# Layer 0 of an attention pair: denominators and output projection put off to the end of the next block

## The chip, the cores and the metric

The kernel runs on one core of a Trainium2 chip. The metric is the device time of one execution in microseconds, the median of several runs; one further execution was recorded by the hardware profiler. Engines are named as in the profile: PE is TensorE (PEld its weight loads), DVE VectorE, ACT ScalarE, POOL GpSimd. All data are fp32.

## The reference

Four images x of 128 channels and 64 x 64 positions (N = 4096) pass two layers. What matters here:

```python
# layer 0: attention over all positions, 64 channels inside
q, k, v = wq @ x, wk @ x, wv @ x                      # 64 x N each
att = softmax(k.T @ q, axis=2)                        # N x N
x = x + wo @ (v @ att.T)                              # projection back to 128 channels
# layer 1: tokens t = x transposed (N x 128)
h = layernorm(t)
t = t + causal_softmax(h Wq (h Wk).T / sqrt(128)) @ (h Wv)
t = t + recurrent_ffn(layernorm(t))                   # batch norm, then a scan over tokens
```

## The kernel before

For each of the four batches, layer 0 handles eight blocks of 512 rows, then layer 1 eight blocks. A block is a list of items; a layer-0 item is two key tiles of 128 (16 items a block), and its scores and values are 64x64 matmuls that occupy the four quarters of the PE array. Layer 1 uses 128x128 matmuls. The softmax isn't normalized until the end: exp of the scores is summed on DVE (`dsum`), and the sums of a block (`den`) are transposed, reduced and inverted later.

PSUM pools: `ps_s` has two score tiles, `ps_a` one accumulator `acc`, and `ps_m` two tiles for everything else; `misc(name)` takes one of the latter, and a tile is free again when its last reader is through.

```python
def misc(name):
    return ps_m.tile([P, BLK], F32, tag="m", name=name)      # pool ps_m: bufs=2
```

The tools' build puts the instructions of each engine into a fixed order, which need not be the order of the source.

The end of a layer-0 block: `acc` is copied out and added up (`agg`), the sums too (`den`); two slots later `project` turns them into the new tokens.

```python
def project(layer, b, g, agg, den):
    dp = misc("den_ps")
    for j in range(TPB):                                        # 4 transposes
        nc.tensor.transpose(dp[:, ts(j, P)], den[:, ts(j, P)], ident)
    rec = recs[:, layer, b, ts(g, TPB)]
    nc.vector.tensor_reduce(rec, dp.rearrange("p (j k) -> p j k", k=P), AX.X, ALU.add)
    nc.vector.reciprocal(rec, rec)
    op = misc("o_ps")
    for j in range(TPB):                                        # 4 matmuls 128x128
        nc.tensor.matmul(op[:, ts(j, P)], lhsT=agg[:, ts(j, P)], rhs=wv1 if layer else wo2, ...)
    for j in range(TPB):
        t = xs[:, b, ds(g * BLK + j * P, P)]
        nc.vector.scalar_tensor_tensor(t, in0=op[:, ts(j, P)], scalar=rec[:, j : j + 1], in1=t, ...)

def transposed(src, dst, name, engine):
    ps = misc(name)
    for j in range(TPB):                                        # 4 transposes
        nc.tensor.transpose(ps[:, ts(j, P)], src[:, j], ident)
    engine(dst, ps)

def finish0(b, g):                                              # layer 0
    agg, den = bs[b].agg, bs[b].den
    ...
    yield 2, lambda: (project(0, b, g, agg, den), norm())       # two slots after the block's end
    fill.append(lambda: transposed(bs[b].xh[...], bs[b].xhT[...], "xhT_ps", nc.scalar.copy))

def values(it):
    ...                                                         # matmuls into bt.acc
    if it.last:
        bt.agg = wk.tile([P, BLK], F32, tag="agg", name="agg")
        if it.layer == 0:
            half = wk.tile([P, 2, BLK], F32, tag="half", name="half")
            nc.scalar.copy(half, bt.acc)
            nc.vector.tensor_tensor(bt.agg, half[:, 0], half[:, 1], ALU.add)
        else:
            nc.scalar.copy(bt.agg, bt.acc[:, 0])
        bt.den = wk.tile([P, BLK], F32, tag="den", name="den")
        nc.vector.tensor_tensor(bt.den, it.den[:, 0], it.den[:, 1], ALU.add)
```

The loop over slots runs scores two items ahead of values:

```python
for s in range(len(items) + SKEW + 16):
    ...
    scores(items[s])                    # PE scores, ACT exp
    it = items[s - SKEW]
    values(it)                          # PE values
    if it.last:
        rows()                          # rows of the block after next; for layer 1 a matmul into r_ps
        if fill:
            fill.pop(0)()               # norm transposes of the preceding block
        push(s, (finish1 if it.layer else finish0)(it.b, it.g))
    sums(items[s])                      # DVE: dsum += p
    ...                                 # then one piece of work that is due
```

So a layer-0 block's projection and layer norm run early in the next block, and the transposes of its normed tokens at the end of that next block.

Of the kernel before, what the change touches and what calls it, by code (L numbers as in the profile page):

```python
# [9 lines left out]
F32 = mybir.dt.float32  # L10
AF = mybir.ActivationFunctionType
ALU = mybir.AluOpType
# [3 lines left out]
P = 128  # L16
BLK = 512
# [325 lines left out]
def fast_path(  # L343
# [21 lines left out]
    nc = tc.nc  # L365
    B, C, N = x.shape
    M = c_wqT.shape[1]
    assert C == P and M == P // 2 and N % CHUNK == 0
    NT = N // P
    NB = N // BLK  # L370
    TPB = BLK // P
# [52 lines left out]
    recs = const.tile([P, 2, B, NT], F32, name="recs")  # L424
# [10 lines left out]
    with tc.tile_pool(name="batch", bufs=1) as batch, tc.tile_pool(name="rows", bufs=2) as rowp, tc.tile_pool(  # L435
        name="prob", bufs=4
    ) as prob, tc.tile_pool(name="work", bufs=2) as wk, tc.tile_pool(name="stat", bufs=4) as stat, tc.tile_pool(
        name="ps_s", bufs=2, space=PSUM
    ) as ps_s, tc.tile_pool(name="ps_a", bufs=1, space=PSUM) as ps_a, tc.tile_pool(
        name="ps_m", bufs=2, space=PSUM  # L440
    ) as ps_m:

        def misc(name):
            return ps_m.tile([P, BLK], F32, tag="m", name=name)
# [69 lines left out]
            nc.vector.tensor_copy(r, ps)  # L514
            bs[b].next.append(r)

        def project(layer, b, g, agg, den):

            dp = misc("den_ps")
            for j in range(TPB):  # L520
                nc.tensor.transpose(dp[:, ts(j, P)], den[:, ts(j, P)], ident)  # L521
            rec = recs[:, layer, b, ts(g, TPB)]
            nc.vector.tensor_reduce(rec, dp.rearrange("p (j k) -> p j k", k=P), AX.X, ALU.add)
            nc.vector.reciprocal(rec, rec)
            op = misc("o_ps")
            for j in range(TPB):
                nc.tensor.matmul(  # L527
                    op[:, ts(j, P)], lhsT=agg[:, ts(j, P)], rhs=wv1 if layer else wo2, start=True, stop=True
                )
            for j in range(TPB):  # L530
                t = xs[:, b, ds(g * BLK + j * P, P)]
                nc.vector.scalar_tensor_tensor(  # L532
                    t, in0=op[:, ts(j, P)], scalar=rec[:, j : j + 1], in1=t, op0=ALU.mult, op1=ALU.add
                )

        def normed(b, g, dst):

            st = stat.tile([P, TPB, nc.vector.BN_STATS_DIM], F32, tag="st", name="ln_st")
            mv = stat.tile([P, TPB, nc.vector.BN_AGGR_DIM], F32, tag="mv", name="ln_mv")
            for j in range(TPB):  # L540
                nc.vector.bn_stats(st[:, j], xs[:, b, ds(g * BLK + j * P, P)])  # L541
                nc.vector.bn_aggr(mv[:, j], st[:, j])
            var = stat.tile([P, TPB], F32, tag="var", name="ln_var")
            nc.vector.tensor_scalar(var, mv[:, :, 1], LN_EPS, None, ALU.add)  # L544
            y = stat.tile([P, TPB], F32, tag="rstd", name="ln_rstd")
            rsqrt(y, var, stat.tile([P, TPB], F32, tag="z", name="ln_z"))
            for j in range(TPB):
                nc.vector.tensor_scalar(  # L548
                    dst[:, j], xs[:, b, ds(g * BLK + j * P, P)], mv[:, j, 0:1], y[:, j : j + 1], ALU.subtract, ALU.mult
                )  # L550
# [14 lines left out]
            nc.vector.tensor_tensor(r, r, r2, ALU.mult)  # L565
            nc.vector.tensor_reduce(good, r, AX.X, ALU.add)

        def finish0(b, g):

            agg, den = bs[b].agg, bs[b].den  # L570

            def norm():
                if g == 0:
                    bs[b].xh = batch.tile([P, NT, P], F32, tag="xh", name="xh")
                    bs[b].xhT = batch.tile([P, N], F32, tag="xhT", name="xhT")
                normed(b, g, bs[b].xh[:, ts(g, TPB)])

            yield 2, lambda: (project(0, b, g, agg, den), norm())
            fill.append(
                lambda: transposed(bs[b].xh[:, ts(g, TPB)], bs[b].xhT[:, ts(g, BLK)], "xhT_ps", nc.scalar.copy)  # L580
            )

        def finish1(b, g):
            agg, den = bs[b].agg, bs[b].den
            mem = {}

            def first():
                project(1, b, g, agg, den)
                mem["xh"] = wk.tile([P, TPB, P], F32, tag="xh2", name="xh2")
                normed(b, g, mem["xh"])  # L590

            def second():
                t = xs[:, b, ts(g, BLK)].rearrange("p (j c) -> p j c", c=P)
                xc = wk.tile([P, BLK], F32, tag="xc", name="xc")
                transposed(t, xc, "tT_ps", nc.scalar.copy)
                nc.sync.dma_start(out=x2[b, :, ts(g, BLK)], in_=xc)
                mem["xhT"] = wk.tile([P, BLK], F32, tag="xhT2", name="xhT2")
                transposed(mem["xh"], mem["xhT"], "xh2T_ps", nc.vector.tensor_copy)

            def third():  # L600
                wp = misc("wx_ps")
                nc.tensor.matmul(wp, lhsT=wf, rhs=mem["xhT"], start=True, stop=True)  # L602
                if b == B - 1 and g == NB - 1:
                    in_range()
                nc.vector.bn_stats(stats[:, b * NB + g], wp)  # L605

                nc.scalar.copy(  # L607
                    xs[:, b, ts(g, BLK)].rearrange("p (s c) -> p s c", c=CPB),
                    wp.rearrange("p (c s) -> p s c", s=STEPS),
                )  # L610

            yield 1, first
            yield 3, second
            yield 1, third
# [84 lines left out]
        def values(it):  # L699

            bt = bs[it.b]
            if it.first:
                bt.acc = ps_a.tile([P, 2, BLK], F32, tag="a", name="acc")
            for h, (t, q0, n, o) in enumerate(it.at):
                if it.layer == 0:

                    for r in range(2):
                        part = slice(r * M, r * M + M)
                        nc.tensor.matmul(  # L709
                            bt.acc[h * M : h * M + M, r],  # L710
                            lhsT=bt.v[part, t],
                            rhs=it.p[part, o : o + n],
                            start=it.first,
                            stop=it.last,
                        )
                else:
                    nc.tensor.matmul(  # L717
                        bt.acc[:, 0, q0:],
                        lhsT=bt.xh[:, t],
                        rhs=it.p[:, o : o + n],  # L720
                        start=it.first and h == 0,
                        stop=it.last and h == 1,
                    )
            if it.last:
                bt.agg = wk.tile([P, BLK], F32, tag="agg", name="agg")
                if it.layer == 0:
                    half = wk.tile([P, 2, BLK], F32, tag="half", name="half")
                    nc.scalar.copy(half, bt.acc)  # L728
                    nc.vector.tensor_tensor(bt.agg, half[:, 0], half[:, 1], ALU.add)
                else:  # L730
                    nc.scalar.copy(bt.agg, bt.acc[:, 0])
                bt.den = wk.tile([P, BLK], F32, tag="den", name="den")
                nc.vector.tensor_tensor(bt.den, it.den[:, 0], it.den[:, 1], ALU.add)

        waiting = []
        fill = []

        def push(slot, chain):
            step = next(chain, None)
            if step:  # L740
                waiting.append((slot + step[0], step[1], chain))
# [13 lines left out]
        side = []  # L755

        def rows():

            if blocks:
                layer, b, g = blocks.pop(0)  # L760
                (rows1 if layer else rows0)(b, g)
                if layer == 0:
                    tokens0(b, g)
# [3 lines left out]
        for s in range(len(items) + SKEW + 16):  # L767
            if s < len(items):
                it = items[s]
                if it.first:  # L770
                    bs[it.b].rows = bs[it.b].next.pop(0)
                    if it.layer and it.g == 1 and it.b + 1 < B:
                        for m in range(NB // 2):
                            side += keys(it.b + 1, m)
                scores(it)
            if 0 <= s - SKEW < len(items):
                it = items[s - SKEW]
                values(it)
                if it.last:
                    rows()  # L780
                    if fill:
                        fill.pop(0)()
                    push(s, (finish1 if it.layer else finish0)(it.b, it.g))
            if s < len(items):
                sums(items[s])
            due = [w for w in waiting if w[0] <= s]
            if due:
                w = min(due, key=lambda w: w[0])
                waiting.remove(w)
                w[1]()  # L790
                push(s, w[2])
            elif side:
                side.pop(0)()
        assert not waiting and not side and not fill

# [143 lines left out]
```

## Time and profile before

| | |
|---|---|
| time, median of 3 runs | 2187.38 us (2187.21 to 2190.06) |
| span of the profiled execution | 2186.7 us |
| granted TensorE clock, mean | 0.989 |
| PE scores, layer 0 (L649) | 4096 instructions, mean 593 ns |
| PE values, layer 0 (L709) | 4096 instructions, mean 590 ns |
| PE transposes den_ps (L521), both layers | 256 instructions, 40.2 us busy |
| PE projection o_ps (L527), layer 0 | 256 instructions, 33.8 us busy |
| PE norm transposes xhT_ps (L556) | 128 instructions, 20.4 us busy |
| ACT copy half (L728) | 32 instructions, about 1003 ns each |
| DVE reduction of den_ps (L523) | 64 instructions, about 684 ns each |
| DVE running sum dsum (L689) | 676 instructions, mean 1225 ns |

Busy time is the sum in which an engine has some instruction at work. The chain that ended last is read backwards from the last instruction, at each step to what released it; its share by engine says who sets the end. A detailed line of the timeline gives start, duration, engine, source line, operation, output and inputs, and in brackets how long the engine had been idle and what ended that. An fp32 matmul that isn't a transpose stands as two instructions in the records.

### The profile page before, as it was taken

The page shows a single profiled execution, that of the slowest core. Times are in us where ns is not written, and L with a number is a line of the kernel's source. Part 1 is how long each engine was busy: PE and PEld are TensorE (multiplying, and loading weights), DVE is VectorE, ACT ScalarE, POOL GpSimd, SP SyncE. Part 2 cuts the span into 40 slices and gives each one's busy share as a digit, 9 for nine tenths or more (in the row PEclk, how much of TensorE's full clock was granted, in tenths as well). Part 3 has the DMA queues.
Part 4 walks back from the last instruction along what each step waited for, and adds up shares of the span by engine and source line. Part 5 has one row for each costly group of instructions (what it writes and reads, how often), then busy time and mean ns, then how long its engine had stood idle before and what let it go on. Part 6 is the DMA issues. An engine that isn't in the chain of part 4 may idle for free.

```text
span 2186.7 us, 30521 instructions
## 1 busy us (share of the span) xinstructions
PE 2113.2 (97%) x12204; PEld 939.7 (43%) x12204; DVE 1440.6 (66%) x2703; ACT 1057.2 (48%) x1162; POOL 104.5 (5%) x207
## 2 busy tenths in 40 slices
PE   6999999999999999999999999999999999999973
PEld 2333354444333345444333335444433334544452
DVE  3888865444788875544688876445478887544486
ACT  4666633333566643333466653332366664332378
POOL 0000010000000010000000001000000001000000
PEclk9999999999999999999999999999999999999986
DMA  6000011000000001000000001100000000000033
GB/s 222 1 1 1 1 31 47 5 6 5 6 1 1 1 20 39 20 10 5 6 1 1 1 1 39 39 6 5 5 6 1 1 1 6 10 10 6 5 159 155
DMA packets 30134, 48.74 MB, mean 22 GB/s; under 512 B 3104, under 2 KB 20256, under 8 KB 28448
## 3 DMA queue, kind: packets, MB, share of 16 engines
q1 hardware_dynamic: 28096, 46.15, 6.1%
q8 instruction: 98, 1.61, 0.3%
q10 hardware_dynamic: 1888, 0.56, 0.1%
q14 instruction: 52, 0.43, 0.1%
HBM read 25.72 MB, written 16.78 MB: 19 GB/s over the span
## 4 chain that ended last, share of the span: by engine, by line
PE 92%; ACT 4%; DVE 2%; DMA 1%; POOL 0%; issue 0%; ACTq 0%; DVEq 0%
PE s_ps L658 21%; PE acc L717 21%; PE s_ps L649 20%; PE acc L709 19%; PE o_ps L527 2%; ACT yt L853 1%; PE den_ps L521 1%; PE kr_ps L469 1%; PE wx_ps L602 1%; ACT xs L841 1%; PE r_ps L512 1%; PE xhT_ps L556 1%; PE v_ps L481 1%; ACT y L841 1%; DVE dsum L689 1%; PE xh2T_ps L556 1%
## 5 line engine op out<-in xcount | busy, mean ns | idle before, releaser
L689 DVE TENSOR_TENSOR dsum<-dsum,p 128x1024 f32<-128x1024 f32 x676 | 828.0, 1225 | 465.6 <-ACT p L665 336.7
L663 ACT ACTIVATE p<-s_ps,nshift 128x1024 f32<-128x1024 f32 x512 | 571.2, 1116 | 354.8 <-PE s_ps L649 335.3
L665 ACT ACTIVATE p<-s_ps 128x1024 f32<-128x1024 f32 (+2 forms) x288 | 274.2, 952 | 564.0 <-PE s_ps L658 462.5
L709 PE MATMUL acc<-p,v 64*64 64x512 f32 x4096 | 532.3, 590 | 1.7 <-ACT half L728 1.7
L649 PE MATMUL s_ps<-swap,kr 64*64 64x512 f32 x2048 | 528.2, 593 | 0.4 <-ACT p L663 0.4
L649 PE MATMUL s_ps<-kr 64*64 64x512 f32 x2048 | 528.2, 593 | 0.0
L658 PE MATMUL s_ps<-rows,xhT 128*128 128x512 f32 (+3 forms) x1152 | 503.9, 559 | 0.0
L717 PE MATMUL acc<-p,xh 128*128 128x512 f32 (+3 forms) x1152 | 501.5, 557 | 0.0
L717 PEld LDWEIGHTS acc<-p,xh 128*128 128x128 f32 x1152 | 215.6, 190 | 241.3 <-issue 231.8
L658 PEld LDWEIGHTS s_ps<-rows,xhT 128*128 128x128 f32 x1152 | 211.0, 190 | 227.1 <-issue 189.7
L709 PEld LDWEIGHTS acc<-p,v 64*64 64x64 f32 x4096 | 155.1, 133 | 284.6 <-issue 265.6
L649 PEld LDWEIGHTS s_ps<-swap,kr 64*64 64x64 f32 x2048 | 136.9, 133 | 130.9 <-issue 123.9
L649 PEld LDWEIGHTS s_ps<-kr 64*64 64x64 f32 x2048 | 137.0, 133 | 128.3 <-issue 123.7
L429 POOL TENSOR_TENSOR ln_rstd<-ln_var,mhalf 128x4 f32<-128x4 f32 x64 | 66.1, 1033 | 1218.6 <-DVE ln_var L544 1218.6
L697 DVE TENSOR_TENSOR dsum<-dsum,p 128x256 f32<-128x256 f32 (+1 forms) x120 | 56.1, 500 | 72.4 <-POOL p L669 72.4
L687 DVE COPY dsum<-p 128x1024 f32<-128x1024 f32 x60 | 41.4, 690 | 67.3 <-ACT p L665 57.6
L532 DVE SCALAR_TENSOR_TENSOR xs<-o_ps,recs,xs 128x128 f32<-128x128 f32 x256 | 73.0, 345 | 8.9 <-PE o_ps L527 2.8
L548 DVE TENSOR_SCALAR xh<-xs,ln_mv,ln_rstd 128x128 f32<-128x128 f32 x256 | 71.4, 343 | 2.2
L669 POOL TENSOR_SCALAR_AFFINE_SELECT p<-p 128x128 f32<-128x128 f32 x128 | 34.4, 292 | 681.7 <-ACT p L665 681.7
L541 DVE BATCH_NORM_STATS2 ln_st<-xs 128x6 f32<-128x128 f32 x256 | 63.7, 273 | 0.0
L840 DVE SCALAR_TENSOR_TENSOR z<-xs,scale,y_ps 128x256 f32<-128x256 f32 x108 | 48.6, 481 | 5.9 <-PE y_ps L838 5.2
L607 ACT COPY xs<-wx_ps 128x512 f32<-128x512 f32 x32 | 18.7, 584 | 69.6 <-DVE stats L605 69.6
(101 smaller groups left out, 1109.2 us busy)
## 6 DMA issues: line engine op xcount, KB each, us to landing
xs<-in_x SPq DMA_DIRECT2D x16, 512.0 KB, 7.2
xs<-in_xT SPq DMA_DIRECT2D x32, 256.0 KB, 3.2
x<-xc SPq DMA_DIRECT2D x32, 256.0 KB, 2.0
xr<-x SPq DMA_DIRECT2D x4, 2048.0 KB, 11.8
out_x<-xr SPq DMA_DIRECT2D x8, 1024.0 KB, 4.0
swap<-kr SPq DMA_DIRECT2D x32, 128.0 KB, 2.2
wo<-in_c_woT ACTq DMA_DIRECT2D x2, 32.0 KB, 4.3
wqT<-in_a_wqT ACTq DMA_DIRECT2D x1, 64.0 KB, 5.9
```

Of the source, the lines that this page charges most:

```text
L429: nc.gpsimd.tensor_tensor(y, var, mhalf[:, : y.shape[-1]], ALU.pow)
L532: nc.vector.scalar_tensor_tensor(t, in0=op[:, ts(j, P)], scalar=rec[:, j : j + 1], in1=t, op0=ALU.mult, op1=ALU.add)
L541: nc.vector.bn_stats(st[:, j], xs[:, b, ds(g * BLK + j * P, P)])
L548: nc.vector.tensor_scalar(dst[:, j], xs[:, b, ds(g * BLK + j * P, P)], mv[:, j, 0:1], y[:, j : j + 1], ALU.subtract, ALU.mult)
L649: nc.tensor.matmul(ps[c * M : c * M + M, off : off + n], lhsT=bs[it.b].kr[part, h, ds(t % (NT // 2) * P + c * M, M)], rhs=rows[h], start=True,
L658: nc.tensor.matmul(ps[:, off : off + n], lhsT=lhsT, rhs=rhs, start=True, stop=True)
L663: nc.scalar.activation(it.p[:, :off], ps[:, :off], AF.Exp, bias=nshift)
L665: nc.scalar.activation(it.p[:, :off], ps[:, :off], AF.Exp, scale=float(P) ** -0.5)
L689: nc.vector.tensor_tensor(flat, flat, it.p, ALU.add)
L697: nc.vector.tensor_tensor(den[:, h, q0:], den[:, h, q0:], it.p[:, o : o + n], ALU.add)
L709: nc.tensor.matmul(bt.acc[h * M : h * M + M, r], lhsT=bt.v[part, t], rhs=it.p[part, o : o + n], start=it.first, stop=it.last,)
L717: nc.tensor.matmul(bt.acc[:, 0, q0:], lhsT=bt.xh[:, t], rhs=it.p[:, o : o + n], start=it.first and h == 0, stop=it.last and h == 1,)
```

## The change

`project` is split into `denominators`, `projected` and `added`. For layer 0, a block's `agg` and `den` are kept in a list `late`; at the end of the next block, the new function `close` transposes the denominators and projects, directly ahead of the norm transposes of the block before that one. The residual add follows, and the norm comes one slot later, so that its transposes fall one block end later than before. The purpose is to gather the 128x128 matmuls of layer 0 in one place per block. For layer 1 `close` does what `values` and the loop did before.

```diff
-        def project(layer, b, g, agg, den):
-
+        def denominators(layer, b, g, den):
             dp = misc("den_ps")
             for j in range(TPB):
                 nc.tensor.transpose(dp[:, ts(j, P)], den[:, ts(j, P)], ident)
             rec = recs[:, layer, b, ts(g, TPB)]
             nc.vector.tensor_reduce(rec, dp.rearrange("p (j k) -> p j k", k=P), AX.X, ALU.add)
             nc.vector.reciprocal(rec, rec)
+
+        def projected(layer, agg):
             op = misc("o_ps")
             ...
+            return op
+
+        def added(layer, b, g, op):
             ...
-        def finish0(b, g):
-            agg, den = bs[b].agg, bs[b].den
-            ...
-            yield 2, lambda: (project(0, b, g, agg, den), norm())
+        def norm0(b, g):
+            ...
+            normed(b, g, bs[b].xh[:, ts(g, TPB)])
             fill.append(
                 lambda: transposed(bs[b].xh[:, ts(g, TPB)], bs[b].xhT[:, ts(g, BLK)], "xhT_ps", nc.scalar.copy)
             )
     ...
+        def close(it, s):
+            bt = bs[it.b]
+            bt.agg = wk.tile([P, BLK], F32, tag="agg", name="agg")
+            if it.layer == 0:
+                half = wk.tile([P, 2, BLK], F32, tag="half", name="half")
+                nc.scalar.copy(half, bt.acc)
+            else:
+                nc.scalar.copy(bt.agg, bt.acc[:, 0])
+            rows()
+            past = late.pop(0) if late else None
+            if past:
+                b, g, agg, den = past
+                denominators(0, b, g, den)
+                op = projected(0, agg)
+            if it.layer == 0:
+                nc.vector.tensor_tensor(bt.agg, half[:, 0], half[:, 1], ALU.add)
+            bt.den = wk.tile([P, BLK], F32, tag="den", name="den")
+            nc.vector.tensor_tensor(bt.den, it.den[:, 0], it.den[:, 1], ALU.add)
+            if fill:
+                fill.pop(0)()
+            if past:
+                added(0, b, g, op)
+                waiting.append((s + 1, lambda: norm0(b, g), iter(())))
+            if it.layer == 0:
+                late.append((it.b, it.g, bt.agg, bt.den))
+            else:
+                push(s, finish1(it.b, it.g))
     ...
                 values(it)
                 if it.last:
-                    rows()
-                    if fill:
-                        fill.pop(0)()
-                    push(s, (finish1 if it.layer else finish0)(it.b, it.g))
+                    close(it, s)
```

More of the change, by code (lines that the diff above doesn't have):

```diff
@@ L532, in project @@
                 nc.vector.scalar_tensor_tensor(
-                    t, in0=op[:, ts(j, P)], scalar=rec[:, j : j + 1], in1=t, op0=ALU.mult, op1=ALU.add
+                    t, in0=op[:, ts(j, P)], scalar=recs[:, layer, b, g * TPB + j : g * TPB + j + 1], in1=t,
+                    op0=ALU.mult, op1=ALU.add,
                 )
@@ L566, in in_range @@
             nc.vector.tensor_reduce(good, r, AX.X, ALU.add)
-        def finish0(b, g):
-            agg, den = bs[b].agg, bs[b].den
[L572 to L576, printed above, removed]
-            yield 2, lambda: (project(0, b, g, agg, den), norm())
+        def norm0(b, g):
+            if g == 0:
+                bs[b].xh = batch.tile([P, NT, P], F32, tag="xh", name="xh")
+                bs[b].xhT = batch.tile([P, N], F32, tag="xhT", name="xhT")
+            normed(b, g, bs[b].xh[:, ts(g, TPB)])
             fill.append(
@@ L587, in first @@
             def first():
-                project(1, b, g, agg, den)
+                denominators(1, b, g, den)
+                added(1, b, g, projected(1, agg))
                 mem["xh"] = wk.tile([P, TPB, P], F32, tag="xh2", name="xh2")
@@ L723, in values @@
                     )
[L724 to L733, printed above, removed]
+        def close(it, s):
[25 more added lines that the diff above has]
+                push(s, finish1(it.b, it.g))
         waiting = []
+        late = []
         fill = []
@@ L793, in fast_path @@
                 side.pop(0)()
-        assert not waiting and not side and not fill
+        assert not waiting and not side and not fill and not late
     with tc.tile_pool(name="xr", bufs=1) as xrp, tc.tile_pool(name="y", bufs=2) as yp, tc.tile_pool(
```

## The prediction

> **What bounds the kernel now.** I read the shares of busy time first, then the chain that ended last, then that chain piece by piece around one block of layer 0, then VectorE and ScalarE over the same microseconds. From the page:
>
> ```profile
> PE 2113.2 (97%) x12204; PEld 939.7 (43%) x12204; DVE 1440.6 (66%) x2703; ACT 1057.2 (48%) x1162; POOL 104.5 (5%) x207
> ...
> PE 92%; ACT 4%; DVE 2%; DMA 1%; POOL 0%; issue 0%; ACTq 0%; DVEq 0%
> ```
>
> TensorE is busy 97% of the span and is 92% of the chain. In a layer-0 stage (31 to 282 us) it is busy 249.56 of 251 us. So a change here counts by what it does to TensorE's sequence: work taken out of it, switches taken out of it, or waits put into it. VectorE and ScalarE count only where TensorE must wait for them.
>
> The chain in order of time (start, duration, piece) at the end of one layer-0 block and the two steps after it:
>
> ```profile
> 91.21 0.86 PE acc L709 x8
> 92.07 0.59 PE xhT_ps L556 x4
> 92.66 1.02 PE s_ps L649 x8
> 93.67 0.86 PE acc L709 x8
> 94.53 0.86 PE s_ps L649 x8
> 95.39 0.86 PE acc L709 x8
> 96.25 0.59 PE den_ps L521 x4
> 96.84 0.89 PE o_ps L527 x8
> 97.73 1.02 PE s_ps L649 x8
> 98.75 0.86 PE acc L709 x8
> ```
>
> An undisturbed step is 0.86 us of scores and 0.86 us of values, both in 64x64 tiles. TensorE leaves them twice per block for work in 128x128 tiles: for the norm transposes (xhT_ps) at the block's end, and for denominators and projection (den_ps, o_ps) two steps later. The same pieces in layer 1, where everything around them is 128x128 already:
>
> ```profile
> 274.32 0.44 PE xhT_ps L556 x4
> ...
> 283.37 1.51 PE s_ps L658 x4
> 284.87 0.89 PE o_ps L527 x8
> ...
> 287.48 0.44 PE den_ps L521 x4
> ```
>
> Four transposes cost 0.44 us there and 0.59 in layer 0, and the scores behind them 1.02 instead of 0.86. So **one detour out of the 64x64 tiles and back costs 0.15 + 0.16 = 0.31 us** beyond its work. Both detours agree: the first lengthens its step by 0.59 + 1.02 - 0.86 = 0.75 = 0.44 + 0.31, the second by 0.59 + 0.89 + 1.02 - 0.86 = 1.64 = 0.44 + 0.89 + 0.31.
>
> VectorE over the same stretch, from the timeline:
>
> ```profile
> 92.42 1.23 DVE L689 TENSOR_TENSOR dsum<-dsum,p 128x1024 f32<-128x1024 f32 x1 [0.87 <-ACT p L663]
> 93.57 0.68 DVE L729 TENSOR_TENSOR agg<-half 128x512 f32<-128x512 f32 x1
> ...
> 96.61 1.22 DVE L689 TENSOR_TENSOR dsum<-dsum,p 128x1024 f32<-128x1024 f32 x1 [0.49 <-ACT p L663]
> 97.75 0.68 DVE L523 TENSOR_REDUCE recs<-den_ps 128x4 f32<-128x512 f32 x1
> ```
>
> Two things are to be seen. The agg add stands before the running sum (dsum) of that step in the source, yet comes behind it: the order in a queue is fixed at build time by what is expected to be ready first. And the reduction of den_ps starts at 97.75 though the denominators were transposed by about 96.84: it stands behind a 1.22 us running sum, and ends at 98.43.
>
> **What the Trainium skill says.** "TensorEngine Tiling (Array Packing)", Key Properties: changing the tiling mode, not merely the tile, drains TensorE. The trace agrees; the price here is 0.31 us for out and back. "PSUM — Partial Sum Buffer", Engine vs sequencer instructions: VectorE's queue is strictly first in, first out, and matmuls start and complete in program order. The trace agrees for the reduction behind the running sum. "Perfetto Trace Analysis", Identifying Performance Opportunities: a gap that repeats on the engine that should be saturated can mean that PSUM or SBUF has no room for the next tile. No such gap is in layer 0 of the kernel before; I expect one after.
>
> **The change, part by part.**
>
> *Removed: detours.* Count places where 64x64 work lies on both sides. Before, per batch: transposes at the ends of blocks 1 to 6 (6) and the denominators and projections of blocks 0 to 6 (7), 13 in all; what falls at the end of block 7 or later lies in layer 1's 128x128 work and costs no switch. After: one common detour at the ends of blocks 1 to 6, 6 in all. 7 x 4 batches x 0.31 = **8.7 us less** if each common detour stays whole. No matmul, transpose or VectorE operation disappears: per batch one projection and one set of transposes only move into layer 1, at their bare cost.
>
> *The half copy.* The next block's first values wait for ScalarE's copy of acc. At the end of block 0, with no detour, the timeline has its last values at 61.27 and the next block's first at 63.59: 2.32 us for a step of 1.72, so 0.6 us lost. From block 1 on, the transposes cover that wait. The common detour covers it as well, so nothing changes there.
>
> *Added: a third tile in a pool of two.* den_ps, o_ps and xhT_ps all come from ps_m, which holds two tiles. Before, one detour used one and the other used two. In the common detour (from block 2 on, when both parts exist) xhT_ps needs the place of den_ps, and this is free only when VectorE has reduced it. Take as zero the start of the block's last values, 91.03 in the timeline. den_ps would begin at 0.97, o_ps at 1.46, and o_ps be issued by about 2.36 (0.49 and 0.9 us later, from the pitches in the existing detour). ScalarE's p of that step ends at 92.39, that is at 1.36; so the running sum is ready before the transposes of den (about 1.63), is put ahead of the reduction and takes until 2.6; the reduction ends at about 3.2 to 3.3. That is what the existing second detour already shows: measured from its own last values (95.21) the reduction ends at 98.43 - 95.21 = 3.22. There nobody waits for it; here TensorE does. **Wait: 3.25 - 2.36 = about 0.9 us** per common detour, against 0.31 saved.
>
> *Sum.* Blocks 2 to 5: (0.9 - 0.31) x 4 x 4 = +9.4 us. Block 6 also has r_ps ahead of den_ps, so four tiles in a pool of two: o_ps waits for the copy of r_ps and xhT_ps for the reduction; I put it at +0.9 net, x 4 = +3.6. The remaining two detours per batch that vanish without a third tile: -0.31 x 2 x 4 = -2.5. Together +10.5 us, so about 2198; I shade it to **2197 us**.
>
> **Rivals.**
>
> *It works as meant: 2179 to 2181.* If the build puts the reduction ahead of the running sum, it ends at about 1.7 + 0.68 = 2.4, just as o_ps is through, and the wait is under 0.1 us: -8.7 plus about 2. For it: the source places the reduction before the running sum of that step, and there is room on VectorE, idle for 0.87 us at 92.42. Against it: the agg add has the same claim by source order and still ran behind the running sum. I give it 0.2.
>
> *The build avoids the wait: about 2185.* It may fill the wait with the next scores and put the transposes behind them. In layer 1 it does so: o_ps at 284.87 comes behind scores, although the denominators that precede it were finished before those, because its place was held by r_ps. Then there are two detours again at blocks 2 to 6, and only 2 x 4 x 0.31 = 2.5 us remain of the saving. I give it 0.1.
>
> *The build cuts the scores in two: about 2202.* The matmuls of a score group run side by side: eight instructions of 593 ns (L649 in the groups) pass in 0.86 us. If the transposes go in after the first or second of them, the group takes two rounds: +0.86, and the 0.31 is not saved. 20 detours x 0.86 - 2.5 = +14.7. I give this 0.25, and the plain wait 0.45. In time they are alike, since the cut group runs while the reduction does.
>
> *VectorE becomes the bound.* At 199.85 of 251 us in layer 0 it is not, and its work is unchanged.
>
> **Range and chances.** About 0.7 for 2194 to 2205, 0.3 for 2178 to 2186: a range of 2179 to 2205 should hold eight in ten. 2% is 44 us; the most favourable sum is 9 us down and the worst some 20 up. Faster by over 2%: 0.01; within 2%: 0.98; slower by over 2%: 0.01.
>
> **What would show it.** Right: in layer 0 one common stretch per block end, with a gap ahead of xhT_ps of 0.5 to 1 us which ends with the reduction of den_ps (L523), itself behind a running sum on VectorE; the old second detour gone; scores at 1.02 once per block instead of twice. Wrong, good for the kernel: reduction ahead of the running sum and no gap. Cut groups would show as score pieces of x2, x4 or x6 with transposes between them. The size of the saving is wrong if the step after a common detour doesn't show 0.31 us less than the two together; the whole is wrong if TensorE gains waits outside the block ends, for instance at the start of layer 1, where one more projection and its norm now fall.

## The result, and the profile after

The changed kernel takes **2201.47 us** (median; 2200.70 to 2204.94) against 2188.36 us for the kernel before on the same chip: a ratio of 1.0062, 95% interval 1.0045 to 1.0080. It is slower by some 13 us; in the two traces the last block of layer 1 ends 12.5 us later. From its page:

```profile
PE 2114.0 (96%) x12204; PEld 947.1 (43%) x12204; DVE 1439.4 (65%) x2703; ACT 1060.1 (48%) x1162; POOL 104.7 (5%) x207
...
PE 12%; ACT 3%; DVE 1%; POOL 0%; issue 0%; ACTq 0%
```

Busy sums have hardly moved: the same work, and a wait more. The chain could be followed back over only 16% of the span here, so I read the waits and the timeline instead. The list of what TensorE waited for has one line that has no counterpart before (us in total, times, longest):

```profile
PE xhT_ps L562 <- DVE recs L522: 12.1, 16, 0.8
```

Sixteen times, four a batch. One of them, the end of block 2 of the first batch, on TensorE:

```profile
118.57 1.04 PE L710 MATMUL acc<-p,v 64*64 64x512 f32 x8
119.54 0.66 PE L520 MATMUL den_ps<-ident,den 128*128 128x128 f32 x4
120.03 1.06 PE L528 MATMUL o_ps<-wo,agg 128*128 128x128 f32 x8
121.84 0.66 PE L562 MATMUL xhT_ps<-ident,xh 128*128 128x128 f32 x4 [0.76 <-DVE recs L522]
122.43 0.65 PE L650 MATMUL s_ps<-swap,kr 64*64 64x512 f32 x2
...
123.34 1.04 PE L710 MATMUL acc<-p,v 64*64 64x512 f32 x8
```

and on VectorE:

```profile
119.96 1.23 DVE L690 TENSOR_TENSOR dsum<-dsum,p 128x1024 f32<-128x1024 f32 x1 [0.88 <-ACT p L664]
121.10 0.69 DVE L522 TENSOR_REDUCE recs<-den_ps 128x4 f32<-128x512 f32 x1
```

All three parts now stand in one stretch. But the transposes begin 3.27 us after the last values instead of 2.36, when the reduction of den_ps ends (121.10 + 0.69 = 121.79), and that stood behind the running sum. From values to values the stretch takes 4.77 us, 3.05 over a plain step of 1.72. Before, the two detours cost 0.75 + 1.64 = 2.39. So each such block end is 0.66 us longer.

Block 6 is different, since r_ps for layer 1 comes first there (first batch, TensorE):

```profile
240.66 1.04 PE L710 MATMUL acc<-p,v 64*64 64x512 f32 x8
...
242.59 0.60 PE L520 MATMUL den_ps<-ident,den 128*128 128x128 f32 x4
243.12 1.07 PE L650 MATMUL s_ps<-kr 64*64 64x512 f32 x2
244.12 1.16 PE L528 MATMUL o_ps<-wo,agg 128*128 128x128 f32 x8
245.11 0.60 PE L562 MATMUL xhT_ps<-ident,xh 128*128 128x128 f32 x4
...
246.98 0.60 PE L710 MATMUL acc<-p,v 64*64 64x512 f32 x3
...
248.69 0.60 PE L710 MATMUL acc<-p,v 64*64 64x512 f32 x3
```

and on VectorE:

```profile
243.19 0.68 DVE L514 COPY rows<-r_ps 128x512 f32<-128x512 f32 x1
243.79 0.68 DVE L522 TENSOR_REDUCE recs<-den_ps 128x4 f32<-128x512 f32 x1
```

r_ps and den_ps fill the pool, so o_ps finds no free place, and the build puts one matmul of the next score group (two instructions) ahead of it. That matmul runs alone for 1 us. The copy of r_ps ends at 243.87, and o_ps follows the score matmul at 244.12; the reduction ends at 244.47, before the transposes begin at 245.11. So TensorE shows no wait here: the cut score group stands in the place of one.

A ledger over the whole kernel: the times at which ScalarE begins to copy acc, one per block, compared between traces. Each number is how much longer than in the kernel before the way is from one such copy to another; the four batches agree within 0.03 us in the first four columns.

| kernel | block 0 to 1 | 1 to 2 | each of 2 to 6 | 6 to 7 | layer 1, batches 0 to 2 | batch 3 |
|---|---|---|---|---|---|---|
| the changed kernel | -1.64 | -0.74 | +0.66 | +0.87 | +2.15 | +1.02 |
| e1, reduction first | -1.64 | -0.75 | -0.20 | +0.88 | +2.92 | +1.79 |
| e2, third place | -1.64 | -0.74 | -0.31 | +0.26 | +2.52 | +1.38 |
| e3, places for both | -1.64 | -0.74 | -0.31 | -0.31 | +2.51 | +1.39 |
| e4, third detour | +0.35 | +0.35 | +0.35 | +0.36 | +1.47 | +2.82 |
| e5, two reductions | -1.64 | -0.74 | +1.31 | +1.02 | +3.21 | +2.09 |
| e7, projection put off alone | -1.64 | -0.75 | 0.00 | +1.19 | +2.91 | +1.82 |

"2 to 6" are the four stretches that follow the ends of blocks 2 to 5; "6 to 7" follows the end of block 6. In layer 1, 0.89 + 0.44 + 0.44 = 1.77 us of every row but e4's is the work that was moved there. The time of the first block's end varies too, by up to 4.0 us between these traces (62.28 us in e5, 62.53 in the kernel before, 66.28 in e7), though no changed piece lies ahead of it; in e7 the scores wait 2.5 us for a transfer there. Medians of kernels therefore differ by a little more or less than their ledgers.

### The profile page after: what moved, and what is told of

The parts are those of the page before. It is cut to its first block, busy times and chain, and to the rows that moved or that the text cites. A ratio compares the mean times of both kernels' runs of the same rounds, so it can differ in the third digit from the quotient of the medians.

```text
span 2198.9 us, 30488 instructions
## 1 busy us (share of the span) xinstructions
PE 2114.0 (96%) x12204; PEld 947.1 (43%) x12204; DVE 1439.4 (65%) x2703; ACT 1060.1 (48%) x1162; POOL 104.7 (5%) x207
## 5 line engine op out<-in xcount | busy, mean ns | idle before, releaser
L710 PE MATMUL acc<-p,v 64*64 64x512 f32 x4096 | 571.2, 590 | 1.7 <-ACT half L733 1.7
L650 PE MATMUL s_ps<-kr 64*64 64x512 f32 x2048 | 567.7, 592 | 0.0
L710 PEld LDWEIGHTS acc<-p,v 64*64 64x64 f32 x4096 | 169.1, 133 | 280.4 <-issue 272.5
L650 PEld LDWEIGHTS s_ps<-kr 64*64 64x64 f32 x2048 | 153.8, 133 | 135.9 <-issue 135.2
## 6 DMA issues: line engine op xcount, KB each, us to landing
xr<-x SPq DMA_DIRECT2D x4, 2048.0 KB, 12.5
```

Of the source, the lines that this page charges most:

```text
L650: nc.tensor.matmul(ps[c * M : c * M + M, off : off + n], lhsT=bs[it.b].kr[part, h, ds(t % (NT // 2) * P + c * M, M)], rhs=rows[h], start=True,
L710: nc.tensor.matmul(bt.acc[h * M : h * M + M, r], lhsT=bt.v[part, t], rhs=it.p[part, o : o + n], start=it.first, stop=it.last,)
```

## The experiments

The theory: xhT_ps waits for a place in ps_m, which den_ps holds until VectorE has reduced it, and VectorE adds a running sum first. The rivals: the long 128x128 stretch as such starves the other engines; putting the projection off costs by itself; detours cost nothing.

**e1: the reduction ahead of the running sum.** One order on VectorE turned round by an ordering edge; TensorE's order is the same as in the changed kernel.

```diff
-                denominators(0, b, g, den)
+                red = denominators(0, b, g, den)       # returns the reduction
+                if it.layer == 0:
+                    ahead.append(red)
...
-                sums(items[s])
+                with tc.issue_after(ahead.pop()) if ahead else ExitStack():
+                    sums(items[s])
```

> The changed kernel with one order turned round: at the end of a layer-0 block VectorE reduces den_ps before it adds that step's running sum. TensorE's order stays the same to the last matmul. Theory (xhT_ps waits for den_ps's place, which the running sum holds up): the wait of 0.8 us at 16 block ends falls to about 0.1, so some 14 us less than the changed kernel, about 2187.5 us; the cut scores at block 6 stay. Rival (the long 128x128 stretch itself starves the other engines): no difference, about 2201.

2192.88 us, ratio to the kernel before 1.0016 (1.0009 to 1.0023). At the end of block 2 of the first batch, VectorE:

```profile
122.03 0.69 DVE L522 TENSOR_REDUCE recs<-den_ps 128x4 f32<-128x512 f32 x1 [1.15 <-PE den_ps L520]
...
123.36 1.20 DVE L691 TENSOR_TENSOR dsum<-dsum,p 128x1024 f32<-128x1024 f32 x1
```

and TensorE:

```profile
120.37 1.04 PE L711 MATMUL acc<-p,v 64*64 64x512 f32 x8
...
121.83 1.06 PE L529 MATMUL o_ps<-wo,agg 128*128 128x128 f32 x8
122.78 0.66 PE L563 MATMUL xhT_ps<-ident,xh 128*128 128x128 f32 x4
...
124.28 1.04 PE L711 MATMUL acc<-p,v 64*64 64x512 f32 x8
```

Now VectorE waits 1.15 us for the denominators, which delays nobody here, and the transposes start 2.41 us after the last values instead of 3.27. The stretch takes 3.91 us instead of 4.77. That is 0.86 us at 16 ends, 13.8 us, as expected. The median was expected at 2187.5 and fell by only some 9 us: by the ledger layer 1 took 0.77 us a batch longer, and the first block's end came 1.8 us later in this trace. The list of TensorE's waits shows where the 0.77 arose (us in total, times, longest):

```profile
PE o_ps L529 <- DVE rows L514: 3.5, 4, 0.9
```

Once a batch, early in layer 1, o_ps of a layer-0 block waits 0.87 us for the place of r_ps, whose copy stands on VectorE behind a layer norm and a running sum. In the changed kernel it waits 0.1 us there. It is the same shortage of places once more. The order of the reduction is the cause of the wait in layer 0; the first rival is out, since the stretch holds the same 128x128 work in the same order and the wait is gone.

**e2: a third place.** xhT_ps of layer 0 goes into a score tile; a score tile is free at that moment.

```diff
-            ps = misc(name)
+            ps = ps_s.tile([P, 2 * BLK], F32, tag="s", name=name)[:, :BLK] if name == "xhT_ps" and spare[0] else misc(name)
```

> The changed kernel with xhT_ps of layer 0 in a place of the score pool ps_s, which is free at that moment; VectorE's order untouched. Theory: no wait at blocks 2 to 5, each 0.98 us shorter, 16 x 0.98 = 15.6; at block 6 no cut scores but o_ps waits about 0.5 us for the copy of r_ps, 4 x 0.7 = 2.7 less. About 2183 us. Rival (it is VectorE's load, not the place): no gain, about 2201. Rival (the score pool is needed): scores wait instead, ScalarE late, gain half of it or less.

2183.99 us, ratio 0.9979 (0.9970 to 0.9987). VectorE still reduces behind the running sum, but nobody waits: blocks 2 to 5 are now 0.31 us shorter than before the change, 0.97 less than in the changed kernel. So either the place or the order cures the wait. At block 6 the build put xhT_ps ahead of o_ps, and o_ps waits for the copy of r_ps (idle before it in brackets):

```profile
239.99 1.16 PE L528 MATMUL o_ps<-wo,agg 128*128 128x128 f32 x8 [0.31 <-DVE rows L514]
```

**e3: a place for r_ps as well.**

```diff
+            spare[0] = it.layer == 0 and it.g == 6      # r_ps in a score tile there
             rows()
+            spare[0] = False
```

> As the run before, and r_ps at the end of block 6 in the score pool as well, so that the common stretch is whole there too (r_ps, den_ps, o_ps, xhT_ps). Theory: block 6 goes from 0.87 us over the kernel before to 0.31 under it, 4 x 1.18 = 4.7 us less than the changed kernel on top of 15.6: about 2181 us, which is 7 under the kernel before and what the change was for. Rival (detours cost nothing once waits are gone): about 2188.

2182.20 us, ratio 0.9967 (0.9956 to 0.9979). The end of block 6 on TensorE, to be held against the block 6 shown above:

```profile
236.90 1.04 PE L712 MATMUL acc<-p,v 64*64 64x512 f32 x8
...
239.26 1.06 PE L530 MATMUL o_ps<-wo,agg 128*128 128x128 f32 x8
240.16 0.60 PE L564 MATMUL xhT_ps<-ident,xh 128*128 128x128 f32 x4
240.69 0.65 PE L652 MATMUL s_ps<-kr 64*64 64x512 f32 x2
...
241.60 1.04 PE L712 MATMUL acc<-p,v 64*64 64x512 f32 x8
```

The whole stretch, r_ps included, takes 4.70 us, and like blocks 2 to 5 it is 0.31 under the kernel before. **This version is faster than both kernels**: 6.4 us under the kernel before. By the ledger the removed detours bring their 7 x 4 x 0.31 = 8.7 us in full, and some 2 us of it go at the start of layer 1. The whole gain had gone into the third place.

**e4: one more detour in the kernel before.** Denominators two slots after the block's end, projection three slots after.

```diff
-            yield 2, lambda: (project(0, b, g, agg, den), norm())
+            yield 2, lambda: project(0, b, g, agg, den, 1)               # denominators only
+            yield 1, lambda: (project(0, b, g, agg, den, 2), norm())     # projection only
```

> The kernel before with its second detour split: denominators two slots after the block's end, projection three slots after. Same work, one more detour out of the 64x64 tiles per block, 7 a batch. Theory (0.31 us for each detour): 28 x 0.31 = 8.7 us more than the kernel before, about 2197 us. Rival (a detour costs only when its work is long, or is hidden): within 2 us of the kernel before.

2206.67 us, ratio 1.0081 (1.0065 to 1.0098): 18 us more, not 9. The first batch, end of block 1:

```profile
97.29 0.66 PE L523 MATMUL den_ps<-ident,den 128*128 128x128 f32 x4
...
98.78 1.04 PE L713 MATMUL acc<-p,v 64*64 64x512 f32 x8
99.75 1.16 PE L530 MATMUL o_ps<-wo,agg 128*128 128x128 f32 x8
```

In layer 0 the expectation holds: every block 0.35 us longer, 28 x 0.35 = 9.9 us. The remaining 7.2 us arose in layer 1 (1.47 three times and 2.82), where the projection of block 7 now falls one slot later; that I had not expected. The waits show part of it, xhT_ps there waiting for the norm four times, 3.5 us in all; the rest I did not resolve. As a price of a detour only the layer-0 columns count.

**e5: two reductions.** The changed kernel with den_ps of layer 0 reduced twice; the first result is thrown away.

```diff
+            if layer == 0:
+                nc.vector.tensor_reduce(stat.tile([P, TPB], F32, tag="extra", name="extra"), dp.rearrange(...), AX.X, ALU.add)
             nc.vector.tensor_reduce(rec, dp.rearrange("p (j k) -> p j k", k=P), AX.X, ALU.add)
```

> The changed kernel with den_ps of layer 0 reduced twice (the first result is thrown away), so that its place comes free about 0.6 us later. The build answers by putting one of the four score matmuls ahead of xhT_ps at blocks 2 to 5 too. Theory (TensorE's time at the block end is set by when the reduction ends, whether it waits or runs part of a score group meanwhile): 0.6 us more at 16 block ends, about 2211 us; block 6, where the reduction ended 0.6 us before it was needed, unchanged. Rival A (a cut score group costs its own 0.86 us on top of the wait): about 2219 or more. Rival B (filling the wait with scores gives the time back): about 2201.

2215.94 us, ratio 1.0122 (1.0105 to 1.0139). At the end of block 2 of the first batch (last values at 118.25), TensorE:

```profile
120.70 1.07 PE L652 MATMUL s_ps<-swap,kr 64*64 64x512 f32 x2
122.22 0.63 PE L564 MATMUL xhT_ps<-ident,xh 128*128 128x128 f32 x4 [0.45 <-DVE recs L524]
```

and VectorE:

```profile
121.39 0.68 DVE L524 TENSOR_REDUCE recs<-den_ps 128x4 f32<-128x512 f32 x1
```

One score matmul fills part of the wait, yet the transposes still start only when the second reduction is through, 3.97 us after the last values. Each of the 16 ends is 1.31 - 0.66 = 0.65 us longer than in the changed kernel, by the 0.6 of one reduction: 10.4 us. Both rivals on the cut group are out: it neither adds its own 0.86 nor gives time back. Block 6 was expected unchanged and is 0.15 us longer: there the second reduction ends at 247.33, just ahead of the transposes at 247.48. The other 4 us lie in layer 1 (1.06 a batch), where o_ps waits 1.09 us for the place of r_ps.

**e7: the projection put off alone**, the transposes in a detour of their own two slots later.

```diff
             if fill:
-                fill.pop(0)()
+                if it.layer == 0:
+                    waiting.append((s + 2, fill.pop(0), iter(())))
+                else:
+                    fill.pop(0)()
```

> One half of the change: denominators and projection are put off to the next block's end, but the norm transposes go two slots later, in a detour of their own, so blocks 2 to 5 never need a third place. Theory: 11 detours a batch against 13 before, 2 x 0.31 less; at block 6 o_ps still waits for r_ps's copy and cuts the scores, about 1.2 more; the start of layer 1 0.4 more: about 0.9 x 4 = 3.8 us over the kernel before, 2192 us. Blocks 2 to 5 exactly as long as before. Rival (putting the projection off costs by itself): near the changed kernel, 2199 or more.

2194.72 us, ratio 1.0025 (1.0014 to 1.0036). Blocks 2 to 5 are as long as before to 0.01 us, and block 6 is 1.19 longer, both as expected. Putting the projection off costs nothing in layer 0 as long as no third tile is asked for at once. Layer 1 took 0.77 us a batch more than in the changed kernel; as in e1, o_ps waits 0.87 us there for the place of r_ps.

## Why the prediction was right, point by point

*The forecast*: 9.6 us more than the kernel before, with a saving of up to 9 us held possible; 13.1 us were measured.

*What bounds it*: right. TensorE's sequence sets the time; VectorE's unchanged work matters in layer 0 only where a tile of ps_m waits for it.

*The price of a detour*: right. 0.31 us by the removal in e2 and e3, 0.35 by the addition in e4, where the projection comes first after the switch and takes 0.10 us longer (1.16 against 1.06).

*Detours removed*: right. The two that vanish without a third tile bring -1.64 - 0.74 + 1.77 = -0.61 us a batch, with the moved work paid back.

*The wait at blocks 2 to 5*: right in kind and place. It was put at 0.9 and is 3.27 - 2.36 = 0.91. The net was put at 0.59 and is 0.66, because the way from the first transpose to the scores takes 0.59 us after a wait (121.84 to 122.43) and 0.53 without one (240.16 to 240.69 in e3). 16 x 0.66 = 10.6 us instead of 9.4.

*Block 6*: the size was right, +0.87 against +0.9, but partly by luck. It had not been worked out, and of the two waits named neither appears: a cut score group fills the time in which o_ps has no place (e2, where no scores stand ahead of it, shows the wait for the copy of r_ps, 0.31), and the reduction ends before xhT_ps needs its place. That the build would cut the scores I had given to a rival, for all blocks; it does so at block 6 alone. That rival charged a cut with 0.86 us in place of the wait; e5 shows that at blocks 2 to 5 the cut fills the wait and adds nothing of its own.

*The mis-sized term*: layer 1's start was put at the bare cost of the moved work. It takes 2.15 us instead of 1.77 in three batches and 1.02 in the last, 3 x 0.38 - 0.75 = +0.4; with 0.36 more between the first two batches that is about +0.7 in all. The sum: 10.6 + 3.5 - 2.5 + 0.7 = 12.3, against 12.5 in the traces. Shading the figure from 2198 to 2197 had no ground. Among the variants of the changed kernel this start lies between +2.51 and +3.21 in the first three batches. There o_ps waits for the place of r_ps: 0.1 us in the changed kernel, 0.30 in e2 and e3, 0.87 in e1 and e7, 1.09 in e5. That is as much as the whole difference from the changed kernel in e1 and e7, nearly all of it in e5, and about half in e2 and e3. It is read from the waits and was not tested by a run of its own; why the copy of r_ps comes so much later in some variants, and where the rest of the changed kernel's own excess comes from, stays open.

*The pages.* "Perfetto Trace Analysis" (Identifying Performance Opportunities) was borne out: the gap that repeats on TensorE, 16 times 0.76 us, was a missing place in PSUM, and e2 shows it by giving one.

## What to carry to other kernels

Gathering work to save switches also gathers its demand for buffers: count how many tiles of a pool the new stretch holds at once, and for the one too many ask when its predecessor's last reader gets its turn in that engine's queue, not how long that reader takes. The gap can be cured on either side, by a free tile elsewhere or by the reader's order. A filler put into the gap by the build saved nothing here, since it broke up a group that was to run side by side.

## What the runs showed of the hardware that was not expected

After a cut the four 64x64 tiles stay out of step through the block that follows, yet lose nothing more: after the cut at the end of block 6 the groups of three value instructions begin at 246.98 and 248.69, 1.71 us apart, the pitch of a plain step. "TensorEngine Tiling (Array Packing)", Key Properties, says that tiles operate independently; the trace agrees. The staggering also misleads the busy sums: the values of layer 0 (L709 before, L710 after) show 571.2 us busy after the change against 532.3 before, with the same mean of 590 ns, because staggered instructions cover more of the time. Those 39 us are no loss; the whole kernel is only 13 us slower.
